# Turned probabilities, blocks and a layernorm dealt out differently in the last batch of a fused attention kernel

## The chip, the cores and the metric

The kernel runs on one core of one Trainium2 chip. The time is what the device needs for one launch, in microseconds; three runs of the kernel before gave 2748.12 us as their median (2746.18 to 2751.13). One launch computes four layers in a row, on eight batches of 512 rows by 512 columns, all in float32.

The engines are named as in the profile: PE is TensorE (its weight loads are shown apart as PEld), DVE is VectorE, ACT is ScalarE, POOL is GpSimd, SP is SyncE, whose queue issues most DMAs. Each engine works through its own instructions in order.

## The reference, cut to what matters

```python
x = L0(x, A_grid, B_grid, dt)        # derivatives of x * A, x * B on a 512 x 512 grid; relu
x = L1(x, mask, timestep, bias, Wq, Wk, Wv, Wo, W1, W2, ...)   # 16 heads of 32
    x = ln(x) * (1 + scale) + shift
    q, k, v = x @ Wq + bq, x @ Wk + bk, x @ Wv + bv
    probs = softmax(where(mask, -inf, q @ k.T / sqrt(32) + bias))
    x = x + (probs @ v) @ Wo + bo
    x = x + gelu2((ln(x) * g2 + beta2) @ W1 + b1) @ W2 + b2
x = L2(x, ...)                       # per batch one of 8 experts: Wi, gelu, Wo, layernorm
x = L3(x, ...)                       # a low-rank response, added with a gate
```

The change touches L0 (its end, and the layernorm that opens L1), the attention of L1, and the layernorm ahead of W1 for batch 0.

## The kernel before, in words

The kernel has three stages. `grid_stage` computes L0 of batch 0. `attention_stage` computes the attention of L1 for all batches, and beside it L0 of batches 1 to 7. `mlp_stage` computes the rest, first the 8 feed-forward parts of L1, then the 8 of L2 with L3 behind each. Between the last two stages the batches lie in DRAM, in `x1d[0]` to `x1d[7]`.

**Units and steps.** Attention is cut into 128 units (b, c, r): batch b, four heads (c = 0 to 3), a quarter of the rows (r = 0 to 3). The loop at L1102 makes one step for each unit, and two more at the end. t = 4c + r is the place of a unit in its batch. In the step of unit `now`, TensorE multiplies the older units' probabilities into the context (`values`, "ctx" in the profile, in every second step, for two quarters at once), then turns (transposes) the probabilities of the unit before, `old`, head by head (`turned`, "tr"), and at the end of the step computes the scores of the next unit (`scores`, "s", one PSUM bank for each of the four heads).

The step has two slots, u = 0 and 1, of two heads each. In each slot come: the turns of `old` and their copies from PSUM to SBUF ("pt"), the softmax of `now` (on VectorE one instruction, which adds scores and bias and takes the minimum, `bt, mn <- s, bt` at L1005; on ScalarE the exponential with its sum, L1010), and then one job of `fill`. The PSUM tiles of the turns have two buffers, so turns 2 and 3 wait for copies 0 and 1. In the last steps of a head group `divide` turns the inverse sums (`rb`, in the same two buffers), ScalarE copies them (`rbs`) and VectorE makes the context `ct`. GpSimd adds the mask to the bias of the next unit (L982).

Instructions wrapped in `pin` keep the order in which the program writes them on their engine. Which engine copies a turn is settled in `turned`: head 0 of a slot goes to VectorE, except in slot 0 at t in (1, 3, 4, 5, 7, 9, 15) (and in the first half of batch 0); all else goes to ScalarE.

**The jobs of `fill`.** For batches before the last they are the q and k blocks of this batch's next head groups, the v, q and k blocks of the next batch, and the output blocks (`o_block`) of the batch before; each block is four matmuls of 128x512 in two halves, one for each slot. The last batch has no next batch: it has q blocks at t = 0, 4, 9, k blocks at 1, 6, 10 and the output blocks of batch 6 at 2, 3, 7, 8, so no block at t = 5 and from 11 on. It prepares the feed-forward of batch 0 instead: statistics at t = 8, `head_norm` (ScalarE) at 10 and 11, and one `head_turn` (a turn on TensorE, an instruction on VectorE) at each of 12 to 15.

**The grid.** L0 of batch n runs beside the attention of the batches before it. It is written as the table `GRID` (L828): row j is done in the step whose index is 16(n-1) - 8 + j, at its end, mostly on VectorE. "s0" and "s1" are the statistics of the two halves of the rows, `grid_pow` makes their inverse root on GpSimd, "n0" and "n1" are the layernorm itself: a small VectorE instruction `gsh` (L817) and two ScalarE activations of 128x512 (L821). n0 stands in row 13, which is t = 5; row 15 is t = 7. `grid_gate` lets GpSimd start its mask adds only behind the last VectorE instruction of the grid in the step before; the table's "n" and "s" entries do not set that gate.

**Loads and stores.** SP's queue carries the bias (three steps ahead), the grid's coefficients, the store of a batch's result to `x1d` (at t = 9 of the batch after) and, in the last batch, `head_load`: batch 0's result at t = 1 and the four quarters of W1 at 3, 5, 11 and behind the last step. The quarters take the homes of batches 4 to 7 in SBUF, so each waits for the store of its batch. The tiles `ct` have five buffers, the grid's coefficient tiles "gq" two and "gc" three.

Of the kernel before, what the change touches and what calls it, by code (L numbers as in the profile page):

```python
# [11 lines left out]
F32 = mybir.dt.float32  # L12
# [8 lines left out]
NB = 8  # L21
S = 512
D = 512
P = 128
# [520 lines left out]
def attention_stage(  # L545
# [12 lines left out]
    nc = tc.nc  # L558
    with ExitStack() as ctx:
        wp = ctx.enter_context(tc.tile_pool(name="aw", bufs=1, reuse_waits="tile"))  # L560
        pp = ctx.enter_context(tc.tile_pool(name="ap", bufs=2, reuse_waits="tile"))
# [63 lines left out]
        def block(out, lhsT, rhs):  # L625

            def half(h):
                for k in (2 * h, 2 * h + 1):
                    mm(out, lhsT(k), rhs(k), k == 0, k == KC - 1)
            return half  # L630
# [49 lines left out]
        def o_block(b, r, tag="m"):  # L680
            o = ps.tile([P, D], F32, name=f"o_{b}_{r}", tag=tag)
            half = block(
                o, lambda k: cts[b, k][:, r * P : (r + 1) * P], lambda k: w["Wo"][:, k, :]
            )
            yield half(0)
            yield half(1)
            pin(nc.vector.tensor_tensor(xt[b][:, r, :], o, xt[b][:, r, :], ALU.add))
# [79 lines left out]
        def grid_op(n, op):  # L767
# [60 lines left out]
        GRID = {  # L828
            0: "q0 q1", 1: "e0 | w0", 2: "c0 hh C0", 3: "+0", 4: "-0 g0", 5: "G0 |", 6: "a0 A0",
            7: "b0 B0", 8: "x0 q2", 9: "e1 | w1 c1", 10: "C1 +1", 11: "-1 g1", 12: "G1 s0",  # L830
            13: "a1 | n0 A1 b1", 14: "B1 x1", 15: "s1", 16: "n1",
        }

        def grid_sums(n, j, late=True, early=True):
# [24 lines left out]
        head, h0, hT0, wi0 = {}, {}, {}, {}  # L859

        def head_load(t):

            if t == 1:
                head["x"] = w8(wo8, "x_0")
                nc.sync.dma_start(head["x"], x1d[0])
            if t in (3, 5, 11, 16):
                g = (3, 5, 11, 16).index(t)
                wi0[g] = xp.tile([P, KC, D], F32, name=f"w1_{g}", tag=f"x{g}", bufs=1)
                load_w1(nc, wi0[g], a, g)

# [24 lines left out]
        def head_turn(c):  # L895
            hT0[c] = io.tile([P, S], F32, name=f"hT0_{c}", tag="x1", bufs=4)
            tr = ps.tile([P, R, P], F32, name=f"h0tr_{c}", tag="m")
            for r in range(R):
                tp(tr[:, r, :], h0[r][:, c * P : (c + 1) * P])
            pin(  # L900
                nc.vector.tensor_scalar(
                    hT0[c], tr.rearrange("f r p -> f (r p)"), g2[:, 0, c : c + 1],
                    g2[:, 1, c : c + 1], ALU.mult, ALU.add,
                )
            )

        def grid_early(j):
            grid_sums(1, j)
            grid_loads(1, j)

        def fill(b, t):

            n = b + 1
            jobs = []
            if b == 0:
                if t == 0:
                    homes = (("m", 1), ("tr", 2), ("tr", 2), ("ctx", 1))
                    for m in range(4):
                        jobs.append(v_block(0, m, *homes[m]))
                        jobs.append(grid_early(j) for j in (m + 3,))  # L920
                    jobs.append(grid_early(7) for _ in range(1))
                    jobs.append(mask_out(0, r) for r in (2, 3))
                elif t == 2:
                    jobs.append(add_bv() for _ in range(1))
                elif t in (3, 4, 6, 7):
                    jobs.append(x1_back(0, (3, 4, 6, 7).index(t)) for _ in range(1))
            if n == NB:
                at = dict(q=(0, 4, 9), k=(1, 6, 10), o=(2, 3, 7, 8))
                for key, f in (("q", q_block), ("k", k_block)):
                    if t in at[key]:  # L930
                        jobs.append(f(b, at[key].index(t) + 1))
                if t in at["o"]:
                    jobs.append(o_block(b - 1, at["o"].index(t)))
            elif t in (0, 4, 8):
                jobs.append(q_block(b, t // 4 + 1))
            elif t in (1, 5, 9):
                turn = (lambda c: x1_in(n, c)) if t == 9 else None
                jobs.append(k_block(b, t // 4 + 1, turn=turn))
            elif t in (2, 3, 6, 7):
                if b:  # L940
                    jobs.append(o_block(b - 1, (2, 3, 6, 7).index(t)))
            elif t == 11:
                jobs.append(q_block(n, 0))
            elif t == 13:
                jobs.append(k_block(n, 0))
            else:
                jobs.append(v_block(n, (10, 12, 14, 15).index(t)))
            if n < NB:
                if t in (11, 12, 13, 14):
                    jobs.append(x1_back(n, t - 11) for _ in range(1))  # L950
                if t >= 12:
                    jobs.append(load_mask(n, t - 12) for _ in range(1))
            elif t == 8:
                jobs.append(head_stats() for _ in range(1))
            elif t in (10, 11):
                jobs.append(head_norm(r) for r in (2 * t - 20, 2 * t - 19))
            elif t >= 12:
                jobs.append(head_turn(t - 12) for _ in range(1))
            for j in jobs:
                yield from j  # L960

# [54 lines left out]
        def turned(b, c, r, u):  # L1016

            bt = bias.pop((b, c, r, u))
            for i in range(2):
                h = 2 * u + i  # L1020
                if r % 2 == 0:
                    pts[b, c, r // 2, h] = pp.tile(
                        [P, KC, 2, P], F32, name=f"pt_{b}_{c}_{r}_{h}", tag=f"pt{h}", bufs=1
                    )
                pt = pts[b, c, r // 2, h]
                tr = ps.tile([P, KC, P], F32, name=f"tr_{b}_{c}_{r}_{h}", tag="tr", bufs=2)
                for k in range(KC):
                    tp(tr[:, k, :], bt[:, i, k * P : (k + 1) * P])
                t = 4 * c + r
                if i == 0 and not (u == 0 and (t in (1, 3, 4, 5, 7, 9, 15) or (b == 0 and t < 8))):  # L1030
                    pin(nc.vector.tensor_copy(pt[:, :, r % 2, :], tr))  # L1031
                else:
                    pin(nc.scalar.copy(pt[:, :, r % 2, :], tr))  # L1033
# [23 lines left out]
        def divide(b, c):  # L1057
            rb = ps.tile([P, R, P], F32, name=f"rb_{b}_{c}", tag="tr", bufs=2)
            for r in range(R):
                tp(rb[:, r, :], sums.pop(("w", b, c, r)).rearrange("p h d -> p (h d)"))  # L1060
            rbs = pp.tile([P, S], F32, name=f"rbs_{b}_{c}", tag="rbs", bufs=1)
            pin(nc.scalar.copy(rbs, rb.rearrange("f r p -> f (r p)")))
            ct = pp.tile([P, S], F32, name=f"ct_{b}_{c}", tag="ct", bufs=5)
            pin(
                nc.vector.tensor_tensor(
                    ct, ctxs.pop((b, c)).rearrange("f r p -> f (r p)"), rbs, ALU.mult
                )
            )
            cts[b, c] = ct
# [32 lines left out]
        for i in range(n + 2):  # L1102
            now = units[i] if i < n else None
            old = units[i - 1] if 1 <= i <= n else None
            two = units[i - 2] if i >= 2 else None
            jobs = fill(now[0], 4 * now[1] + now[2]) if now else iter(())
            grid_gate(i)
            if i + 1 < n:
                add_mask(*units[i + 1])
            grid_step(i - 1, grid_pow)  # L1110
            pair = two and two[2] % 2 == 1
            if pair:
                values(two[0], two[1], two[2] // 2)
            for u in range(2):
                if old:
                    turned(*old, u)
                if now:
                    softmax(*now, u)
                next(jobs, None)
            drain(jobs)  # L1120
            split = pair and two[2] == R - 1
            if split:
                grid_step(i, lambda n, j: grid_sums(n, j, late=False))
                divide(two[0], two[1])
            if old:
                inverse(*old)
            if i + 3 < n:
                load_bias(*units[i + 3])
            if now and now[0] == NB - 1:
                head_load(4 * now[1] + now[2])  # L1130
            if now and now[0] and now[1:] == (2, 1):
                nc.sync.dma_start(x1d[now[0] - 1], xt[now[0] - 1])
            grid_step(i, lambda n, j: grid_sums(n, j, early=not split))
            grid_step(i, grid_loads)
            if i + 1 < n:
                scores(*units[i + 1])
# [753 lines left out]
```

## Time and profile before

The profiled execution took 2746.39 us, its span, from the first to the last instruction, 2744.6 us.

| stretch (us from the start) | length | PE busy | DVE busy | ACT busy | POOL busy | granted PE clock |
|---|---|---|---|---|---|---|
| grid of batch 0, first weights: 0 to 71.2 | 71.2 | 52.8 | 52.7 | 16.2 | 26.0 | 0.93 |
| attention of batches 0 to 6: 71.2 to 968.6 | 897.4 | 884.1 | 764.8 | 616.3 | 506.8 | 1.00 |
| attention of batch 7 and its end: 968.6 to 1105.5 | 136.9 | 129.0 | 74.5 | 81.9 | 60.1 | 0.98 |
| feed-forward parts: 1105.5 to 2744.6 | 1639.1 | 1627.8 | 1007.6 | 319.7 | 912.3 | 1.00 |

A row says for how many us of the stretch each engine had an instruction running. Matmuls are pipelined, so a busy TensorE is not one at its peak. The granted clock is a share of full speed.

The steps of batch 7 begin, by their first TensorE instruction, at 968.58 (t = 0), 974.98, 983.69, 990.09, 998.36, 1004.77, 1011.79, 1018.25, 1026.52, 1032.92, 1041.63, 1048.04, 1055.49, 1061.73, 1069.85 and 1076.40 (t = 15). The two closing steps follow, the first of the last output blocks' matmuls starts at 1091.74 and the first matmul of the feed-forward at 1105.47.

### The profile page before, as it was taken

To read this page: it belongs to the slowest core of one execution; us is meant where nothing else is said; L and a number is where in the kernel's file an instruction comes from. 1 tells how busy PE (TensorE), PEld (TensorE's weight loads), DVE (VectorE), ACT (ScalarE), POOL (GpSimd) and SP (SyncE) were. 2 spreads that over 40 slices of the span, in tenths; PEclk is the share of its full clock that TensorE was granted. 3 is DMA by queue.
4 is the path that set the end of the run, shared out by engine and by line. 5 is a ranking of instruction groups with operands and counts; after the bars stand their busy time and mean duration, and the time that the engine had idled before them with its cause. 6 is when DMAs were issued, how large, how long until landed. Compare 5 with 4: busy or idle time off the path is not lost.

```text
span 2744.6 us, 39872 instructions
## 1 busy us (share of the span) xinstructions
PE 2693.7 (98%) x14662; PEld 2007.0 (73%) x14662; DVE 1899.7 (69%) x3506; ACT 1034.0 (38%) x2196; POOL 1505.3 (55%) x1091
## 2 busy tenths in 40 slices
PE   7999999999999998999999999999999999999998
PEld 4455555555555555888888888888888888888886
DVE  7888888888888655677656756665456566566564
ACT  2576767667667765211211211211121221221221
POOL 3455555555555653565555656646546636636633
PEclk9999999999999999999999999999999999999998
DMA  8765767666675544642543344253133143143120
GB/s 318 238 222 178 246 190 232 220 194 227 195 242 180 170 155 142 192 129 54 143 143 84 96 145 124 55 173 123 44 127 131 51 150 128 53 150 103 63 70 31
DMA packets 190208, 405.27 MB, mean 148 GB/s; under 512 B 24024, under 2 KB 28704, under 8 KB 183742
## 3 DMA queue, kind: packets, MB, share of 16 engines
q1 hardware_dynamic: 186202, 391.97, 42.7%
q0 software_dynamic: 3360, 10.68, 3.2%
q8 instruction: 117, 1.92, 0.3%
q14 instruction: 77, 0.63, 0.1%
q10 hardware_dynamic: 452, 0.07, 0.0%
HBM read 366.97 MB, written 31.50 MB: 145 GB/s over the span
## 4 chain that ended last, share of the span: by engine, by line
PE 92%; DVE 4%; ACT 2%; DMA 1%; issue 1%; SPq 0%; ACTq 0%; POOL 0%; DVEq 0%
PE u L1173 28%; PE y L1173 28%; PE tr L570 8%; PE s L567 5%; PE ctx L567 4%; PE pq L567 4%; PE pv L567 4%; PE o L567 4%; PE pk L567 3%; PE btr L1176 1%; DVE bt L1005 1%; PE xb L570 1%; DVE x L695 1%; PE ytr L1176 1%; ACT bt L1010 1%
## 5 line engine op out<-in xcount | busy, mean ns | idle before, releaser
L982 POOL TENSOR_TENSOR bt<-bt,mk 128x1024 f32<-128x1024 f32 x256 | 542.6, 2141 | 56.8 <-DMA bt<-in_bias 38.2
L1173 PE MATMUL y<-wo,act 128*128 128x256 f32 x2560 | 573.3, 380 | 0.0
L1173 PEld LDWEIGHTS y<-wo,act 128*128 128x128 f32 x2560 | 481.3, 190 | 70.0 <-issue 6.9
L1010 ACT ACTIVATE bt<-bt,mn 128x512 f32<-128x512 f32 x512 | 365.7, 716 | 78.6 <-DVE mn L1005 78.0
L570 PEld LDWEIGHTS tr<-ident,bt 128*128 128x128 f32 x2048 | 229.1, 141 | 153.0 <-issue 124.7
L1005 DVE CUSTOM_DVE_ANT_0 bt<-s,bt 128x512 f32<-128x512 f32 x512 | 330.8, 684 | 2.4 <-PE s L567 2.4
L1173 PE MATMUL u<-bt,wi 128*128 128x256 f32 x1440 | 330.5, 379 | 0.0
L1179 DVE TENSOR_TENSOR act<-u,u 128x512 f32<-128x512 f32 x256 | 173.3, 686 | 210.0 <-PE u L1173 132.6
L1173 PEld LDWEIGHTS u<-bt,wi 128*128 128x128 f32 x1440 | 273.5, 190 | 37.2
L570 PE MATMUL tr<-ident,bt 128*128 128x128 f32 x2048 | 276.2, 278 | 11.5 <-ACT pt L1033 9.4
L1173 PE MATMUL u<-tb,ws 128*128 128x256 f32 x1024 | 242.2, 379 | 0.0
L1033 ACT COPY pt<-tr 128x512 f32<-128x512 f32 x315 | 177.1, 581 | 159.6 <-PE tr L570 155.7
L1173 PE MATMUL y<-t,s 128*128 128x256 f32 x1024 | 234.2, 380 | 0.0
L1182 POOL TENSOR_TENSOR t<-wo,t 128x512 f32<-128x512 f32 x64 | 106.6, 1681 | 200.6 <-PE y L1173 200.5
L1173 PEld LDWEIGHTS u<-tb,ws 128*128 128x128 f32 x1024 | 194.3, 190 | 26.6 <-DVE tb L1179 0.2
L1031 DVE COPY pt<-tr 128x512 f32<-128x512 f32 x197 | 135.7, 689 | 112.7 <-PE tr L570 98.0
L1173 PEld LDWEIGHTS y<-t,s 128*128 128x128 f32 x1024 | 191.1, 190 | 24.1
L1493 ACT ACTIVATE act<-act,b 128x512 f32<-128x512 f32 x128 | 82.9, 712 | 292.9 <-DVE act L1179 292.9
L1493 ACT ACTIVATE act<-act,bi 128x512 f32<-128x512 f32 x128 | 83.8, 712 | 282.6 <-DVE act L1179 282.6
L1179 DVE TENSOR_TENSOR x<-y,x 128x512 f32<-128x512 f32 x96 | 64.5, 685 | 159.1 <-PE y L1173 105.2
L1179 DVE TENSOR_TENSOR u<-u,u 128x512 f32<-128x512 f32 x192 | 131.3, 684 | 58.2 <-PE u L1173 58.1
L567 PE MATMUL s<-kt,qt 32*128 32x512 f32 x1024 | 166.4, 640 | 2.5 <-DVE mn L1005 1.6
(316 smaller groups left out, 4250.1 us busy)
## 6 DMA issues: line engine op xcount, KB each, us to landing
bt<-in_bias SPq DMA_DIRECT2D x256, 512.0 KB
wo<-in_W SPq DMA_DIRECT2D x32, 1024.0 KB
wi<-in_Wi SPq DMA_DIRECT2D x32, 1024.0 KB
wo<-in_Wo_e SPq DMA_DIRECT2D x32, 1024.0 KB
wi<-in_W SPq DMA_DIRECT2D x28, 1024.0 KB
gq<-coef_q SPq DMA_DIRECT2D x21, 512.0 KB
x1d<-x SPq DMA_DIRECT2D x8, 1024.0 KB
x<-x1d SPq DMA_DIRECT2D x8, 1024.0 KB
```

What stands on the lines that cost most here:

```text
L567: pin(nc.tensor.matmul(out, lhsT=lhsT, rhs=rhs, start=start, stop=stop))
L570: pin(nc.tensor.transpose(out, src, ident))
L982: nc.gpsimd.tensor_tensor(bt, bt, mask[b, r][:, None, :].to_broadcast([P, 2, S]), ALU.add)
L1005: nc.vector.tensor_tensor_reduce(bt[:, i, :], ss[h], bt[:, i, :], -1.0, 3.0e38, ALU.add, ALU.min, mn)
L1010: nc.scalar.activation(bt[:, i, :], bt[:, i, :], AF.Exp, bias=mn, scale=-1.0, accum_out=sums[b, c, r][:, h : h + 1],)
L1031: pin(nc.vector.tensor_copy(pt[:, :, r % 2, :], tr))
L1033: pin(nc.scalar.copy(pt[:, :, r % 2, :], tr))
L1173: pin(nc.tensor.matmul(out, lhsT=lhsT, rhs=rhs, start=start, stop=stop))
L1176: pin(nc.tensor.transpose(out, src, idn))
L1179: pin(nc.vector.tensor_tensor(out, x, y, op))
L1182: pin(nc.gpsimd.tensor_tensor(out, x, y, op))
L1493: nc.scalar.activation(acts[g][:, k, :], acts[g][:, k, :], func, bias=bi[:, j : j + 1])
```

## The change

Four things are rearranged; no computation is added or left out.

1. n0 moves from row 13 of `GRID` to row 15, ahead of s1.
2. In the last batch a turn is copied by ScalarE only if it is head 1 of slot 0; the other three go to VectorE. The rule for the other batches is the old one.
3. The last batch's ten q, k and o blocks come out of one generator, `halves`, in the order q1, k1, q2, k2, o0, q3, k3, o1, o2, o3, one half at a time: two halves at t = 0, 7, 8, 11, 12 and 14, none at 13 and 15, one elsewhere. The turns of h come in pairs at t = 13 and 15.
4. As batch 6's output blocks end later, its store to `x1d` goes from t = 9 to t = 15, and the load of the third quarter of W1 behind it; and the last batch's `ct` tiles take the buffers "gq" and "gc", which the grid no longer uses.

```diff
-            13: "a1 | n0 A1 b1", 14: "B1 x1", 15: "s1", 16: "n1",
+            13: "a1 | A1 b1", 14: "B1 x1", 15: "n0 s1", 16: "n1",
...
-            if t in (3, 5, 11, 16):
-                g = (3, 5, 11, 16).index(t)
+            if t in (3, 5, 15, 16):
+                g = (3, 5, 15, 16).index(t)
...
+        def halves(b):
+
+            for g in (
+                q_block(b, 1), k_block(b, 1), q_block(b, 2), k_block(b, 2), o_block(b - 1, 0),
+                q_block(b, 3), k_block(b, 3), *(o_block(b - 1, r) for r in (1, 2, 3)),
+            ):
+                next(g)
+                yield
+                for _ in g:
+                    pass
+                yield
...
             if n == NB:
-                at = dict(q=(0, 4, 9), k=(1, 6, 10), o=(2, 3, 7, 8))
-                for key, f in (("q", q_block), ("k", k_block)):
-                    if t in at[key]:
-                        jobs.append(f(b, at[key].index(t) + 1))
-                if t in at["o"]:
-                    jobs.append(o_block(b - 1, at["o"].index(t)))
+                if t == 0:
+                    head["fill"] = halves(b)
+                jobs.append(
+                    next(head["fill"], None)
+                    for _ in range({0: 2, 7: 2, 8: 2, 11: 2, 12: 2, 13: 0, 14: 2, 15: 0}.get(t, 1))
+                )
...
-            elif t >= 12:
-                jobs.append(head_turn(t - 12) for _ in range(1))
+            elif t in (13, 15):
+                jobs.append(head_turn(c) for c in (t - 13, t - 12))
...
-                if i == 0 and not (u == 0 and (t in (1, 3, 4, 5, 7, 9, 15) or (b == 0 and t < 8))):
+                scalar = i == 1 or (
+                    u == 0 and (t in (1, 3, 4, 5, 7, 9, 15) or (b == 0 and t < 8))
+                )
+                if b == NB - 1:
+                    scalar = i == 1 and u == 0
+                if not scalar:
                     pin(nc.vector.tensor_copy(pt[:, :, r % 2, :], tr))
                 else:
                     pin(nc.scalar.copy(pt[:, :, r % 2, :], tr))
...
-            ct = pp.tile([P, S], F32, name=f"ct_{b}_{c}", tag="ct", bufs=5)
+
+            tag, bufs = (("gq", 2), ("gc", 3))[c // 2] if b == NB - 1 else ("ct", 5)
+            ct = pp.tile([P, S], F32, name=f"ct_{b}_{c}", tag=tag, bufs=bufs)
...
+            if now and now[0] and now[1:] == ((2, 1) if now[0] < NB - 1 else (3, 3)):
+                nc.sync.dma_start(x1d[now[0] - 1], xt[now[0] - 1])
             if now and now[0] == NB - 1:
                 head_load(4 * now[1] + now[2])
-            if now and now[0] and now[1:] == (2, 1):
-                nc.sync.dma_start(x1d[now[0] - 1], xt[now[0] - 1])
```

## The prediction

> **What bounds the kernel now.** The page comes first. Its first part shows a kernel bound by TensorE; its groups give the price of the three operations that the change trades.
>
> ```profile
> PE 2693.7 (98%) x14662; PEld 2007.0 (73%) x14662; DVE 1899.7 (69%) x3506; ACT 1034.0 (38%) x2196; POOL 1505.3 (55%) x1091
> ...
> L1005 DVE CUSTOM_DVE_ANT_0 bt<-s,bt 128x512 f32<-128x512 f32 x512 | 330.8, 684 | 2.4 <-PE s L567 2.4
> ...
> L1033 ACT COPY pt<-tr 128x512 f32<-128x512 f32 x315 | 177.1, 581 | 159.6 <-PE tr L570 155.7
> ...
> L1031 DVE COPY pt<-tr 128x512 f32<-128x512 f32 x197 | 135.7, 689 | 112.7 <-PE tr L570 98.0
> ```
>
> The softmax minimum takes 684 ns on VectorE, a copy of turned probabilities 689 ns there and 581 ns on ScalarE. The shares are means over stages, so the second view is a table of stretches, one for each step of the last batch; I number its steps t=0 to 15. A step starts with its first TensorE instruction: "ctx" in odd steps, "tr" in even ones.
>
> ```profile
> core 0: us, PE busy (x) PEld busy (x) DVE busy (x) ACT busy (x) POOL busy (x), PEclk, DMA share, GB/s
> ...
> 1018.25:1026.52 8.27, 8.27 (x69) 4.35 (x65) 4.59 (x12) 4.86 (x13) 3.31 (x2) 1.00 0.43 126
> 1026.52:1032.92 6.40, 6.40 (x36) 3.40 (x32) 4.18 (x11) 4.73 (x12) 0.00 (x0) 1.00 0.55 161
> ...
> 1048.04:1055.49 7.45, 6.87 (x61) 3.66 (x57) 3.82 (x11) 5.99 (x14) 6.66 (x4) 1.00 0.92 338
> 1055.49:1061.73 6.24, 5.43 (x29) 3.06 (x28) 4.54 (x12) 5.65 (x15) 5.16 (x3) 1.00 0.74 224
> ...
> 1082.42:1087.03 4.61, 2.94 (x17) 2.40 (x17) 1.82 (x7) 2.67 (x7) 0.00 (x0) 0.70 0.02 5
> 1087.03:1091.25 4.22, 4.22 (x34) 2.07 (x33) 0.03 (x1) 0.78 (x2) 0.00 (x0) 0.52 0.00 0
> ```
>
> A step with a whole q, k or o block (t=7, 8) keeps TensorE full and takes 8.27 (odd) or 6.40 us (even). Steps t=11, 12 have no block, so some 3.4 us less of matmuls, and still take 7.45 and 6.24. So something else bounds a step at about the same length. The third view, VectorE's instructions in order of time in t=8, shows what:
>
> ```profile
> 1026.71 0.69 DVE L1005 CUSTOM_DVE_ANT_0 bt<-s,bt 128x512 f32<-128x512 f32 x1 [0.39 <-PE s L567]
> ...
> 1027.33 0.69 DVE L1005 CUSTOM_DVE_ANT_0 bt<-s,bt 128x512 f32<-128x512 f32 x1
> ...
> 1029.81 0.69 DVE L1031 COPY pt<-tr 128x512 f32<-128x512 f32 x1 [1.78 <-PE tr L570]
> 1030.41 0.68 DVE L1005 CUSTOM_DVE_ANT_0 bt<-s,bt 128x512 f32<-128x512 f32 x1
> ...
> 1031.02 0.69 DVE L1005 CUSTOM_DVE_ANT_0 bt<-s,bt 128x512 f32<-128x512 f32 x1
> ```
>
> **The loop of a step.** Back to back, VectorE starts one of these each 0.60 to 0.62 us. The third turn starts 2.65 us into the step (two turns 0.93, a half block 1.72), its copy 0.64 later, then two minima; the last ends 5.19 in. Score matmul 3 of the next unit needs that minimum (its bank). In t=14 the minimum ends at 1075.29, that matmul is issued at 1075.34 and the next step starts at 1076.40: 0.05 and 1.06. In t=8 TensorE itself reaches the scores at 5.33, so VectorE is 0.1 us early: the cover is that thin.
>
> **Part 1, turned probabilities of the last batch.** The order of instructions shows 23 copies leave ScalarE for VectorE (25 become 48); each step copies turns 0, 2 and 3 on VectorE, in the order copy 0, min 0, min 1, copy 2, copy 3, min 2, min 3. Copies 2 and 3 both stand ahead of minima 2 and 3. So with a half block in the first slot the last minimum ends at 5.19 + 0.60 = 5.79, and an even step lasts 5.79 + 0.05 + 1.06 = **6.90**; an odd one has 1.87 us of ctx ahead, **8.77**. The freed 0.58 us of ScalarE buys nothing: exponentials wait for minima. Copy 0 (ready 0.69 in, then min 0, 1 until 2.6) hides under the 2.65 until turn 2; if it did not, up to 0.7 more a step.
>
> A rule speaks against this move: the Trainium skill, "Advanced Engine Details and Errata", section "The Read-Write Bubble", says that ScalarE is nearer to PSUM and VectorE nearer to SBUF. The rows agree, 581 against 689 ns. Priced by the rule alone, the swap costs 23 x 0.11 = 2.5 us of engine time, maybe none on the path. Priced by its place, 14 steps carry a third copy at 0.60 = 8.4 us, less the thin cover. I take the place.
>
> **Part 2, blocks by halves.** It adds no matmul. Halves: two in t=0, 7, 8, 11, 12, 14, none in 13, 15, else one, always in the first slot, ahead of turns 2 and 3. Thus even a one-half step has turn 2 at 2.65, and 6.90 / 8.77 holds for it although its matmuls would need only 4.69 / 6.55; for two halves TensorE needs 6.40 / 8.27, also less than the loop. Extra: in t=4 q2's eviction falls between min 1 and copy 2 (half ends 2.81, eviction starts 2.85, next op 3.52 instead of 3.29): +0.23, 7.13. In t=13 a turn of h (0.60 us) replaces the half, but its eviction (0.72 from start to start in t=14) holds copy 2 to 3.24: end 5.69, 8.70 with ctx. The statistics in t=8 (3.2 us), `ct` and late evictions run after the last minimum and delay only copy 0, under its cover.
>
> Sum t=1 to 14: 6 x 8.77 + 8.70 + 6 x 6.90 + 7.13 = 109.85. Before: 1076.40 - 974.98 = 101.42. **+8.4 us.** t=0 turns the batch before by the old rule: 0.
>
> **Part 3, the tail.** From t=15 to the first o matmul took 15.34 us. Redone with the new order: copy 2 of unit 15 done at 5.8, so the last unit's turns start 5.85 in (6.02 before); min 3, h's eviction and `rs` to 8.4, copy 0 to 9.1, turn 2 at 9.13 (8.75 before); copies 2 and 3 now both on VectorE end at 11.1 (11.31 before, on ScalarE). About -0.2. The last two rows above show the granted clock at 0.70 and 0.52. The Trainium skill, "TensorE: Matmul & The Clock Gate", Part 1, puts the half clock behind an idle window of about 3.4 us; here the longest idle piece was 1.67 us and the clock fell all the same, so the page's condition is too narrow. By the page the new tail (idle pieces up to 2.2) would run at full clock, 1.7 us shorter; by the row it falls again, and if later, up to 1.7 us of the o matmuls are hit. I take the row: 0, both ends kept.
>
> **Part 4, n0 two steps later.** In batches 1 to 6 step t=6 loses TensorE time to it:
>
> ```profile
> 892.13 0.68 DVE L1005 CUSTOM_DVE_ANT_0 bt<-s,bt 128x512 f32<-128x512 f32 x1
> 892.26 1.07 PE L570 MATMUL tr<-ident,bt 128*128 128x128 f32 x8 [0.70 <-ACT pt L1033]
> ```
>
> ScalarE's two activations (1.52) stood ahead of both first copies; t=6 took 7.61 instead of 6.40. But VectorE in that step is back to back from 889.12 (`ct`, rs, gsh, grid ops 1.13 each, then minima) until 895.25, and the scores end 1.11 later at 896.36. When the 0.70 goes, that wait stands in its place: the gain is gsh's 0.05. Batch 0 gives 0.2 (an idle 0.16 of VectorE). At its new place, end of t=7, gsh meets GpSimd's four mask adds (8.43 us from 900.59). It took 0.13 us 13 times of 14, but 1.24 when an add was running, ending with that add. Here it would wait 0.4 (904.41 to the add's end at 904.81); VectorE has 0.64 idle in t=8: hidden. The activations end about 906.5, copies 907.05 and 907.6, just ahead of turns at 907.33 and 907.8. **-0.5**, ends -6.0 (7 x 0.86, if the gap were the whole loss) and +11 (gsh misses one add).
>
> **Part 5, DMA.** x1d[6] is stored at the end of t=15, after o3, and w1_2 waits for it on SP. Queued behind are only the b2 row, x1d[7], the Gram-Schmidt inputs and w1_3: no bias load. x1d[7]'s store to w1_3's issue took 4.34 us before, so w1_2 is issued some 4 us into t=15; GpSimd first reads it 11.6 us into the MLP (1117.10 - 1105.47), over 20 us later. `ct` in the grid's idle buffers: no wait. h turned in pairs: counted. Cost 0; without cover, a few us.
>
> **Sum.** +8.4 - 0.5 - 0.1 = +7.8 us on the profiled 2746.39 (span 2744.6 and 1.79 around it) = 2754.2. The median shown is 1.73 higher; on it, 2755.9.
>
> **Rivals.**
> - The copy hides and TensorE's work decides: then one-half steps fall to 4.69 / 6.55 (0.53 more with rb), t=1 to 14 to 88.9: -12.5, 2735. It decides if the last minimum ends before TensorE reaches the scores, 3.6 us into an even one-half step; seven VectorE ops at 0.61 need 4.3 alone. For it: the empty steps' idle is real. 0.06.
> - n0's gap is the whole loss (-6): 2750, no change. Against it: the back-to-back row. 0.12.
> - gsh loses the race with an add in each batch: 2.1 later, less 0.8 cover, 1.3 to 1.7 each: 2766. Against it: the one case seen was granted at the add's end. 0.07.
> - The change doesn't do what it says: excluded by the order (VectorE +23 rows, ScalarE -23).
>
> **The numbers.** Forecast 0.75, own range 2752 to 2759 (tail clock 1.7 each way, copies 0.52 to 0.69). 0.2%, what a measurement can tell, is 5.5 us. Forecast lies above it but for 0.05. So faster 0.06, same 0.17, slower 0.77. Range 2748.5 to 2761 leaves out the first and third rival and some edges.
>
> **What would show it.** Right: steps of about 6.9 and 8.8 us from t=1 to 14, scores waiting for DVE mn in each; t=6 of batches 1 to 6 still near 7.5 with the wait moved from ACT pt to DVE mn. Wrong: one-half steps near 4.7 / 6.6, t=6 at 6.4, or mask adds and gsh of over 1 us at t=7.

## The result and the profile after

| | before | after |
|---|---|---|
| median of 5 runs | 2748.12 us (2746.18 to 2751.13) | 2760.66 us (2756.26 to 2760.98) |
| profiled execution | 2746.39, span 2744.6 | 2756.26, span 2754.5 |
| mean granted clock | 0.994 | 0.993 |

The ratio is 1.0036, 95% interval 1.0025 to 1.0047: slower by 0.36%, or 9.9 us from profile to profile and 12.5 between the medians. The forecast was 2756.0, in a range of 2748.5 to 2761.0.

First the page of after: busy time of the engines, and the groups that answer to those shown of before.

```profile
PE 2708.8 (98%) x14662; PEld 2012.7 (73%) x14662; DVE 1919.5 (70%) x3529; ACT 1022.2 (37%) x2173; POOL 1505.6 (55%) x1091
...
L1017 DVE CUSTOM_DVE_ANT_0 bt<-s,bt 128x512 f32<-128x512 f32 x512 | 330.8, 683 | 1.3 <-PE s L567 1.3
...
L1048 DVE COPY pt<-tr 128x512 f32<-128x512 f32 x220 | 149.9, 688 | 109.8 <-PE tr L570 101.5
L1050 ACT COPY pt<-tr 128x512 f32<-128x512 f32 x292 | 164.7, 582 | 156.3 <-PE tr L570 153.2
```

The 23 copies have moved (197 to 220, 315 to 292) at unchanged durations. TensorE has the same 14662 instructions and is busy 15.1 us longer. A busy engine that does the same work in more time is either waiting inside a group of matmuls or clocked lower. The table of stretches, one row a step of the last batch, tells the two apart.

```profile
core 0: us, PE busy (x) PEld busy (x) DVE busy (x) ACT busy (x) POOL busy (x), PEclk, DMA share, GB/s
...
998.91:1007.72 8.81, 8.10 (x29) 4.09 (x28) 5.16 (x13) 3.81 (x11) 4.74 (x3) 0.81 0.43 122
...
1016.49:1023.38 6.89, 6.40 (x29) 3.32 (x28) 5.17 (x14) 4.86 (x13) 4.33 (x3) 1.00 0.51 154
1023.38:1033.82 10.44, 10.44 (x66) 5.17 (x65) 5.10 (x13) 3.82 (x11) 2.53 (x2) 0.84 0.34 100
1033.82:1040.71 6.89, 6.89 (x33) 3.69 (x32) 5.52 (x13) 3.65 (x10) 0.00 (x0) 1.00 0.50 153
...
1092.00:1095.40 3.40, 1.99 (x13) 1.26 (x12) 3.40 (x10) 1.79 (x7) 0.00 (x0) 1.00 0.93 307
1095.40:1098.80 3.40, 2.02 (x16) 1.15 (x17) 2.59 (x6) 1.48 (x5) 0.00 (x0) 1.00 0.22 84
```

These are t=4, 6, 7 and 8 and two pieces of the tail. Even steps take 6.89 whether they hold one half block (t=6) or two (t=8): what bounds them isn't TensorE's work. Steps t=4 and t=7 are longer than their like by 1.9 and 1.7 us, and there the clock is 0.81 and 0.84. In the tail, where it had been 0.70 and 0.52, it is 1.00. (A granted clock between 0.5 and 1 in a row is a mean: in these traces it is always either full or half.) VectorE's instructions in order of time, in t=10, show the bound:

```profile
1052.76 1.29 DVE L1048 COPY pt<-tr 128x512 f32<-128x512 f32 x2 [0.38 <-PE tr L570]
1053.97 0.68 DVE L1017 CUSTOM_DVE_ANT_0 bt<-s,bt 128x512 f32<-128x512 f32 x1
...
1054.57 0.69 DVE L1017 CUSTOM_DVE_ANT_0 bt<-s,bt 128x512 f32<-128x512 f32 x1
```

The step started at 1049.48. Copies 2 and 3 run one after the other from 3.28 on, and only then come minima 2 and 3; the last ends 5.78 into the step (5.19 before). TensorE's timeline shows the wait for it, and what follows such a wait:

```profile
997.25 1.73 PE L567 MATMUL s<-kt,qt 32*128 32x512 f32 x4 [0.49 <-DVE mn L1017]
998.91 1.37 PE L570 MATMUL tr<-ident,bt 128*128 128x128 f32 x8
1000.08 3.34 PE L567 MATMUL pq<-x,Wq 128*128 128x512 f32 x4
...
1023.38 3.60 PE L567 MATMUL ctx<-pt,v 128*32 128x256 f32 x32
```

Four score matmuls are spread over 1.73 us; then the four matmuls of pq take 3.34 instead of 1.88, and in t=7 ctx takes 3.60 instead of 1.93: the granted clock is at half for one stretch of 3.41 us each, called half clock below.

Where the 9.9 us between the profiles are: t=1 to 14 took 113.15 us (before 101.42), of which 3.35 are the excess of the two low-clock steps (1.68 of t=4 over its forecast 7.13, 1.67 of t=7 over 8.77), so **+8.4 for the loop and +3.4 for the clock**; the tail from t=15 to the first o matmul is 13.48 (15.34), **-1.9**; the last batch begins **0.5** earlier; from the MLP's first matmul to the end it is **0.5** longer. 8.4 + 3.35 - 1.9 - 0.5 + 0.5 = 9.9.

### The profile page after: what moved, and what is told of

The parts are those of the page before. It is cut to its first block, busy times and chain, and to the rows that moved or that the text cites. A ratio compares the mean times of both kernels' runs of the same rounds, so it can differ in the third digit from the quotient of the medians.

```text
span 2754.5 us, 39872 instructions
## 1 busy us (share of the span) xinstructions
PE 2708.8 (98%) x14662; PEld 2012.7 (73%) x14662; DVE 1919.5 (70%) x3529; ACT 1022.2 (37%) x2173; POOL 1505.6 (55%) x1091
## 4 chain that ended last, share of the span: by engine, by line
PE 95%; DVE 3%; DMA 1%; issue 0%; ACT 0%; SPq 0%; ACTq 0%; POOL 0%; DVEq 0%
PE u L1192 28%; PE y L1192 28%; PE tr L570 8%; PE s L567 6%; PE ctx L567 4%; PE o L567 4%; PE pq L567 4%; PE pk L567 4%; PE pv L567 3%; PE btr L1195 1%; PE l L251 1%; PE rb L570 1%; PE ytr L1195 1%; PE xb L570 1%; DVE bt L1017 0%; DMA a<-in_A 0%
## 5 line engine op out<-in xcount | busy, mean ns | idle before, releaser
L1048 DVE COPY pt<-tr 128x512 f32<-128x512 f32 x220 | 149.9, 688 | 109.8 <-PE tr L570 101.5
L1050 ACT COPY pt<-tr 128x512 f32<-128x512 f32 x292 | 164.7, 582 | 156.3 <-PE tr L570 153.2
L567 PE MATMUL s<-kt,qt 32*128 32x512 f32 x1024 | 181.3, 643 | 3.5 <-DVE mn L1017 2.7
```

What stands on the lines that cost most here:

```text
L567: pin(nc.tensor.matmul(out, lhsT=lhsT, rhs=rhs, start=start, stop=stop))
```

## The experiments

Each ratio below is to runs of the kernel before on the same chip (2749.6 to 2749.9 us), with its 95% interval.

**Parts alone.** Three kernels take one part of the change each. The copies on the kernel before:

```diff
-                if i == 0 and not (u == 0 and (t in (1, 3, 4, 5, 7, 9, 15) or (b == 0 and t < 8))):
+                scalar = i == 1 or (
+                    u == 0 and (t in (1, 3, 4, 5, 7, 9, 15) or (b == 0 and t < 8))
+                )
+                if b == NB - 1:
+                    scalar = i == 1 and u == 0
+                if not scalar:
```

> The kernel before with part 1 alone: in the last batch the copies of turns 0, 2 and 3 go to VectorE and that of turn 1 to ScalarE; whole blocks, n0, the order of turned h as before. Loop theory (copy 3 stands ahead of the last two minima): about +6.5 us over the kernel before, from steps with a block at 6.9 (even) and 8.8 us (odd) instead of 6.4 and 8.3, and from the steps without a block (t=5, 11 to 14), where VectorE is the bound already, each about 0.6 longer; up to 5 more or less if the clock's half windows fall elsewhere. Rival (dealing the blocks by halves is what costs): no difference, within 1 us of the kernel before.

Measured: 2755.57 us, 1.0022 (1.0013 to 1.0031), +5.7. Its t=1 to 14 took 110.54 us: 8.77 and 6.90 in most steps with a block, 7.99 in t=5 (7.02 before). Half clock left the tail and fell in t=11 to 14 (three stretches). The copies cost without any halves.

The halves, on the changed kernel (copies and n0 undone):

```diff
-            13: "a1 | A1 b1", 14: "B1 x1", 15: "n0 s1", 16: "n1",
+            13: "a1 | n0 A1 b1", 14: "B1 x1", 15: "s1", 16: "n1",
...
-                scalar = i == 1 or (
-                    u == 0 and (t in (1, 3, 4, 5, 7, 9, 15) or (b == 0 and t < 8))
-                )
-                if b == NB - 1:
-                    scalar = i == 1 and u == 0
-                if not scalar:
+                if i == 0 and not (u == 0 and (t in (1, 3, 4, 5, 7, 9, 15) or (b == 0 and t < 8))):
```

> The changed kernel with the copies of the last batch by the old rule and n0 back at its old step, so the blocks by halves (with h turned in pairs, ct in the grid's buffers and the later store of x1d) alone. Loop theory: steps of about 6.3 and 8.2 us with one half, 6.4 and 8.3 with two, so about +0.5 us over t=1 to 14 and over the kernel before; the evenly filled steps may keep the clock up in the tail, up to 1.9 us less. Rival (halves are the cost): +8 us.

Measured: 2746.32 us, 0.9987 (0.9979 to 0.9996), a gain of 3.6. Steps of 6.30 and 8.17 with one half (6.52 in t=4), 6.40 and 8.27 with two; t=1 to 14 took 101.95 us, 0.53 over before as expected. No half clock fell in the last batch, and the runs spread over 2.4 us instead of 6.7. At the same mean clock, 0.994, the runs of the kernel before took 2746.7 us on average and those of this kernel 2746.3; but only 7 of 47 runs of the kernel before had a clock of 0.994 or more, and 9 of these 13. So dealing the blocks evenly pays through the clock, by more than was allowed for, and the price lies elsewhere.

n0 alone, on the kernel before:

```diff
-            13: "a1 | n0 A1 b1", 14: "B1 x1", 15: "s1", 16: "n1",
+            13: "a1 | A1 b1", 14: "B1 x1", 15: "n0 s1", 16: "n1",
```

> The kernel before with part 4 alone, n0 two steps later. Theory: -0.5 us, because the wait of 0.70 for the two first copies is replaced by one for VectorE's minima; step t=6 of batches 1 to 6 stays near 7.5 us. Rival (the gap was the whole loss): -6 us, t=6 at 6.4 to 6.8.

Measured: 2748.25 us, 0.9995 (0.9987 to 1.0004): no difference that can be told, and -6 (0.9978) lies outside. Step t=6 took 7.54 us (7.61 before). In the changed kernel the same step of batch 6 shows where the wait went:

```profile
891.00 1.04 PE L570 MATMUL tr<-ident,bt 128*128 128x128 f32 x8
...
893.68 2.28 PE L567 MATMUL s<-kt,qt 32*128 32x512 f32 x8
...
893.49 0.68 DVE L1017 CUSTOM_DVE_ANT_0 bt<-s,bt 128x512 f32<-128x512 f32 x1
...
894.09 0.69 DVE L1017 CUSTOM_DVE_ANT_0 bt<-s,bt 128x512 f32<-128x512 f32 x1
```

The turns no longer wait for ScalarE's copies (0.70 before). The scores, which take 1.14 us where nothing holds them up, are drawn out to 2.28, while VectorE is still at minima 2 and 3; they end 1.18 us after the last minimum.

The parts don't add up: +5.7, -3.6 and -1.6 make +0.5, while the whole change comes to +9.9 by its ratio (1.0036, from another set of runs). The steps show how they work against each other. Halves win nothing where the loop of VectorE is the bound: they put a half block ahead of turn 2 in the formerly empty steps too (t=5 8.77 instead of 7.99), and with the same work spread thin over longer steps the half clock appears in t=4 and t=7.

**Place or amount.** Copy 3 back on ScalarE, copy 0 stays moved:

```diff
                 if b == NB - 1:
-                    scalar = i == 1 and u == 0
+                    scalar = i == 1
```

> The changed kernel with the copy of turn 3 of the last batch back on ScalarE: 16 of the 23 moved copies go back, the other 7 (turn 0) stay on VectorE. Place theory (only what stands ahead of the last two minima costs): steps of 6.3 and 8.2, the whole 8 us go, within 1.5 us of the kernel before. Amount theory (VectorE's load costs wherever it stands): 7 of 23 of the loss stay, +3 to +4 us.

Measured: 2745.77 us, 0.9987 (0.9981 to 0.9994). The loop takes as long as with the halves alone, to 0.01 us (101.95), so the seven copies of turn 0 cost nothing, and the sixteen of turn 3 cost it all. The time is 4.1 below the kernel before, more than the 1.5 expected, because no half clock fell in the last batch here either. VectorE's timeline of t=10, which starts at 1042.66 here:

```profile
1045.94 0.69 DVE L1048 COPY pt<-tr 128x512 f32<-128x512 f32 x1 [0.38 <-PE tr L570]
1046.55 0.68 DVE L1017 CUSTOM_DVE_ANT_0 bt<-s,bt 128x512 f32<-128x512 f32 x1
...
1047.16 0.69 DVE L1017 CUSTOM_DVE_ANT_0 bt<-s,bt 128x512 f32<-128x512 f32 x1
```

Copy 2 starts 3.28 into the step as in the changed kernel, but the first late minimum at 3.89 instead of 4.49: one copy less ahead of it, 0.60.

The other way round, all copies stay on VectorE and only their order changes:

```diff
-                    pin(nc.vector.tensor_copy(pt[:, :, r % 2, :], tr))
+                    copy = lambda pt=pt, tr=tr: pin(nc.vector.tensor_copy(pt[:, :, r % 2, :], tr))
...
+                if u == 1 and not scalar and b == NB - 1:
+                    late.append(copy)
+                else:
+                    copy()
...
                 if now:
                     softmax(*now, u)
+                for copy in late:
+                    copy()
```

> The changed kernel with one order turned round: in the last batch VectorE takes the minima of heads 2 and 3 ahead of the copies of turns 2 and 3, with the same copies on the same engines. Loop theory: the scores no longer wait for copies, a one-half step falls toward TensorE's own 4.7 (even) and 6.6 us (odd), t=1 to 14 to some 92 us instead of 113, no half clock there: about -10 us against the kernel before (2738 to 2742). Rival (VectorE's amount of work, 48 copies, is the cost): no gain over the changed kernel, +8 to +11 us against the kernel before.

Measured: 2742.21 us, 0.9976 (0.9967 to 0.9985), 7.4 below the kernel before with the very copies that had cost 8: it is their place, not VectorE's load. The size was too hopeful: t=1 to 14 took 98.6 us, not 92. Even one-half steps came to 4.93 (t=4 to 5.93), odd ones stayed at 6.9 to 8.4, and half clock fell in t=13 and 14 and again in the tail.

The same order in all batches (the condition without `b == NB - 1`):

> As the run before, with the minima of heads 2 and 3 ahead of the copy of turn 2 in all eight batches. Where TensorE is full nothing changes; in step t=6, which waits for VectorE's minima since n0 was moved, the wait gets 0.6 shorter in seven batches: 0 to -4 us against the run with the last batch alone. Rival: the later copies hold up ctx in the odd steps, up to +0.6 in each of some 50 steps, so slower by several us.

Measured: 2733.11 us, 0.9942 (0.9928 to 0.9955). That is 9 us less than with the last batch alone, where at most 4 were expected: a batch of 1 to 6 takes 124.51 us instead of 125.78, because t=2 falls from 7.54 to 6.54 as well as t=6 to 6.59; t=7 gives 0.6 back. In t=2 the scores had waited for the same minima, behind two of the grid's operations on VectorE; the expectation had reckoned with t=6 only. What still holds odd steps up is seen in TensorE's timeline of t=1:

```profile
972.60 1.04 PE L570 MATMUL tr<-ident,bt 128*128 128x128 f32 x8
974.49 0.66 PE L570 MATMUL rb<-ident,rw 128*128 128x128 f32 x4 [0.85 <-DVE pt L1048]
975.07 1.14 PE L567 MATMUL s<-kt,qt 32*128 32x512 f32 x8
```

and in VectorE's:

```profile
973.13 0.69 DVE L1017 CUSTOM_DVE_ANT_0 bt<-s,bt 128x512 f32<-128x512 f32 x1
...
973.75 1.28 DVE L1048 COPY pt<-tr 128x512 f32<-128x512 f32 x2
```

The scores follow without a wait now, but rb needs a bank of the turns, and those are freed by the two copies that were put last. That asks for one late copy instead of two.

**The best version.** Order first in all batches, and copy 3 of the last batch on ScalarE (both edits above):

> Minima of heads 2 and 3 first in all batches, and the copy of turn 3 of the last batch back on ScalarE. In the run with the order alone, the turn of the row sums (rb) waited 0.8 us in odd steps for the last of two late copies on VectorE, and ctx is next in line. Theory: with one late copy instead of two these waits shrink by up to 0.6 in the odd steps, -1 to -4 us against that run, 2729 to 2732. Rival: copy 3 now stands ahead of the exponentials of heads 2 and 3 on ScalarE, and what is won is lost to late turns: no difference, or +1 to +2.

Measured: 2729.42 us, 0.9932 (0.9919 to 0.9946): 20 us below the kernel before and 3.7 below the last run (on another chip; the intervals overlap, and so, barely, do the single runs, 2728.62 to 2731.17 against 2730.86 to 2734.24). Its rb of t=1 still waits:

```profile
972.15 0.66 PE L570 MATMUL rb<-ident,rw 128*128 128x128 f32 x4 [0.73 <-ACT pt L1050]
```

now for ScalarE, and t=1 is only 0.12 shorter, while t=2 grew by 0.17. Between the two profiles, 4.9 us apart, t=1 to 14 gave 1.7, mostly in t=9 (8.38 to 7.97) and t=13 (8.72 to 7.59), and the tail 1.6, where the half clock is gone. Another 2.2 lie ahead of the last batch, where the two kernels are alike and half clock lasted 3.4 us instead of 6.8 in batch 0: that part is luck. The MLP took back 0.6. So the time lies within what was expected, but the waits that the expectation named gave little of it.

**What the halves are worth then.** The order alone on the kernel before, in the last batch and in all:

> The kernel before with the minima of heads 2 and 3 of the last batch ahead of the copy of turn 2, nothing else. It tells what the blocks by halves are good for. Loop theory: only the steps without a block (t=5, 11 to 14) can get shorter, until ScalarE (5.7 to 6 us of work in t=11 and 12) bounds them: -3 to -5 us; but TensorE has little work in these steps, and half windows of the clock will fall there and give back 1.7 us each. Rival (halves don't matter): as far below the kernel before as the changed kernel with this order, -10 us.

> The kernel before with one change, the minima of heads 2 and 3 ahead of VectorE's copy of turn 2 in all batches: whole blocks, old copies, old n0. With the run of the same order on the changed kernel with copy 3 on ScalarE it tells what the blocks by halves are worth once the order is right. Theory: batches 1 to 6 as there, 1.2 us less each and about 8 in sum, the last batch as in the run with that order in the last batch alone (-6): -14 us against the kernel before, so 6 us are left to the halves, mostly because steps without a block are bounded by ScalarE's work. Rival (the order alone is all): -20 us.

Measured: 2743.74 us, 0.9981 (0.9975 to 0.9988) and 2734.70, 0.9944 (0.9930 to 0.9957): -5.9 (a little more than the 3 to 5 expected) and -15.0. The empty steps got shorter by 0.6 each (t=11 6.85, t=12 5.65, t=13 7.59, t=14 5.88), and one stretch of half clock fell in the tail of each. The step after the empty t=5 grew by the 0.6 that t=5 had lost (t=6 7.07). So the order is worth 15 us, and the halves with copies that don't stand in the way some 3 to 5 more (0.9932 against 0.9944, 2729.42 against 2734.70; these intervals overlap too, but the single runs do not: 2728.62 to 2731.17 against 2733.15 to 2735.55).

**n0 once more.** Its gap, so the argument went, was hidden under the late minima. With the order first in all batches, n0 went back to its old step:

> Minima of heads 2 and 3 first in all batches, with n0 at its old step. Theory: moving n0 won little because VectorE's minima were as late as ScalarE's copies; with the minima no longer late, the old place costs its gap again in t=6, 0.7 to 1.0 us in each of seven batches: +5 to +7 us against the run with n0 moved. Rival (n0's place never matters): within 1 us of it.

Measured: 2734.09 us, 0.9947 (0.9934 to 0.9961), against 0.9942 with n0 moved: the rival was right. The wait for ScalarE's first copies is back in t=6 of batch 6, but it is 0.35 long, and a batch takes 124.58 us (124.51). The first line below is from t=6 with n0 in its old place, the second from t=7 with it moved:

```profile
883.47 1.06 PE L570 MATMUL tr<-ident,bt 128*128 128x128 f32 x8 [0.35 <-ACT pt L1050]
...
894.32 0.66 PE L570 MATMUL tr<-ident,bt 128*128 128x128 f32 x4 [0.43 <-ACT pt L1050]
```

Step t=6 takes 6.94 and t=7 8.63 with n0 in its old place, 6.59 and 8.92 with it moved. The move shifts a third of a microsecond from one step to the next.

**The clock.** Is the 3.4 us of t=4 and t=7 a matter of the clock, and can work in the waits prevent it? Twelve transposes of the identity (1.4 us) were added to the steps with at most one half, into banks that the scores overwrite. At first they stood between the score matmuls:

```diff
+                if b == NB - 1 and i < 3 and 4 * c + r in (2, 3, 4, 5, 6, 7, 10, 11, 14):
+                    for k in range(KC):
+                        tp(s[:, k * P : (k + 1) * P], ident)
                 mm(
                     s, qs[b, c][o : o + HD, r * P : (r + 1) * P], ks[b, c][o : o + HD, :],
...
```

> The changed kernel with 12 more transposes of the identity (1.4 us) ahead of the first three score matmuls of each step with at most one half block in t=1 to 13, written to banks that the scores then overwrite. They stand where TensorE would wait for VectorE. Theory (the second part of the loss is the clock, halved after a stretch with little work in the array): the steps stay at 6.9 and 8.8, no half windows in t=4 and t=7, so -2 to -4 us against the changed kernel, some 2754.5 at a small spread. Rival (more work on the busiest engine costs its time): 9 x 1.4, +12 us; or no change, if the clock isn't set by the amount of work.

Measured: 2772.21 us, 1.0084 (1.0071 to 1.0098), about 13 us over the changed kernel by the ratios, as the rival said; but most of the nine steps had grown by 1.5 to 2.5 us, more than the 1.4 that was added, and TensorE's timeline shows why:

```profile
990.37 1.04 PE L570 MATMUL tr<-ident,bt 128*128 128x128 f32 x8
991.24 0.60 PE L570 MATMUL s<-ident 128*128 128x128 f32 x4
991.77 1.12 PE L567 MATMUL s<-kt,qt 32*128 32x512 f32 x2
992.82 0.66 PE L570 MATMUL s<-ident 128*128 128x128 f32 x4
993.41 1.12 PE L567 MATMUL s<-kt,qt 32*128 32x512 f32 x2
```

One head's score (x2) takes 1.12 us, and all four (x8) took 1.14: on 32 rows each they run beside each other, which the transposes between them forbid. The experiment measured that, not the clock. With all twelve ahead of the first score:

```diff
+            warm = b == NB - 1 and 4 * c + r in (2, 3, 4, 5, 6, 7, 10, 11, 14)
...
+            for i in range(3 * warm):
+                for k in range(KC):
+                    tp(two[i % 2][:, k * P : (k + 1) * P], ident)
             for i in range(4):
...
```

> The changed kernel with the 12 transposes of the identity again, now all ahead of the first score matmul of the step (in the banks of heads 0 and 1, which are free early), so that the four score matmuls still run beside each other. Clock theory: TensorE is through with them at about 5.0 us into an even step, before the last minimum at 5.8; the steps stay at 6.9 and 8.8, no stretch of t=1 to 13 has little work, no half windows there: -2 to -4.5 us against the changed kernel, 2756 to 2758.5. Rival: each step gets longer by the added 1.4 us, +12 us.

Measured: 2755.62 us, 1.0024 (1.0014 to 1.0034), some 3.3 below the changed kernel by the ratios, spread over 1.4 us instead of 4.7. The intervals overlap (up to 1.0034 here, from 1.0025 there), so the times alone are weak; the steps decide:

```profile
998.41 1.47 PE L570 MATMUL s<-ident 128*128 128x128 f32 x12
999.81 2.04 PE L567 MATMUL s<-kt,qt 32*128 32x512 f32 x8
1001.79 0.44 PE L570 MATMUL tr<-ident,bt 128*128 128x128 f32 x2
```

This is t=3. The added work ends before the last score's minimum and the step stays at 8.77. All of t=1 to 14 took 110.20 us, against 113.15 without it; t=4 takes 7.11 and t=7 8.77, at full clock. The two profiled executions nevertheless took the same time (2756.22 and 2756.26), because the last batch began 2.8 us later in this one, behind batches in which the two kernels are alike. So the steps show that more work on the busiest engine made the last batch shorter, by 2.9 us; that the whole kernel gains as much rests on the ratios.

## Why the prediction was right, and where its size was off

- **The loop (part 1).** Right, and to the tenth: 109.85 us were forecast for t=1 to 14. Take the clock's 3.35 off the measured 113.15 and 109.80 remain; with the clock kept up, 110.20. Even steps 6.89, odd 8.77, t=13 8.71. That place and not engine time sets the price is shown from both sides, by copy 3 alone (all the loss goes with it) and by the order (the copies stay, the loss goes). The Trainium skill's "The Read-Write Bubble" ("Advanced Engine Details and Errata") names the right direction, 582 ns on ScalarE against 688 here, but priced by it the part would have cost 2.5 us at most.
- **Halves (part 2).** "6.90 / 8.77 holds for it" was right. t=4 was forecast at 7.13 and is 7.11 where the clock stays up.
- **The tail (part 3): the step that failed is the one on the clock.** The forecast took the row of the old tail, expected the half clock there again and set 0. It left the tail, 1.9 us shorter, and went to two places in the loop, 3.35 us longer. Net +1.5 in the profile. For the tail the branch that was not taken gave the right number: by the idle window of the Trainium skill ("TensorE: Matmul & The Clock Gate", Part 1) the tail was to run at full clock, 1.7 shorter, and 0.2 came from the new order. But that condition does not give the loop, where TensorE idled for 0.49 us in each of the two stretches ahead of half clock. Why the clock stayed up in this tail is open. The row was the right witness against the condition of an idle window, but I read it as a property of the tail, not of the amount of work, and never asked it of the steps that the same sum had just stretched.
- **n0 (part 4).** The mechanism was right: t=6 takes 7.54 and waits for the minima instead of the copies, and a batch of 1 to 6 takes 125.78 us instead of 125.85, some 0.4 in all, where the forecast had 0.3 for these batches and 0.2 for batch 0. That the last batch also begins 0.49 earlier is luck: over the ten profiles with the old order in batches 0 to 6 it begins at 968.1 to 970.9, and most of that spread is in batch 0, where the half clock that falls there lasted 6.8 us in all six profiles with n0 moved and 3.4 in the four without. Whether n0's place does that isn't shown. gsh took 0.43 us at its new place in batches 1 to 6 (0.4 forecast) and 1.60 in batch 0; GpSimd's adds did not cost a step. The reason given, that only VectorE's lateness hid a larger gain, fell: with the minima early, n0's place is worth 0.07 us a batch.
- **DMA (part 5).** No wait for the later store showed. Up to 1631 us into the MLP its matmuls come 0.2 us earlier than before; the 0.5 by which the MLP is longer arise in its last 8 us, where half clock falls in both. What makes the difference there isn't shown; over all 14 profiles the MLP takes 1639.0 to 1640.0.
- **The sum.** 2754.2 for the profiled execution, measured 2756.26; 2755.9 for the median, measured 2760.66. That is 0.3 inside the upper end of the range, and outside the narrower 2752 to 2759 that went with the forecast. The first gap of 2.1 is the clock (+1.5) and the MLP (+0.5). The second is wider because the profiled run of after was the fastest of its five: the others ran at a mean clock of 0.991 or 0.992 against 0.993. A thousandth of the mean over 2750 us is 5.5 us at half clock, 2.75 us of TensorE's work, so by this estimate the step from 0.993 to 0.991 is worth up to 5.5; it was 4.4 to 4.7. I carried the 1.73 us between profile and median of before over; in after this distance was 4.4. Over the 47 later runs of before, with a median of 2749.89, it would have been 3.5: the profiled run of before was a fast one as well.
- **Rivals.** "The copy hides and TensorE's work decides" came true only once the order was changed, and "n0's gap is the whole loss" is refuted by n0 alone. The third, gsh losing its race with an add in each batch, did not come: 0.43 us in each of batches 1 to 6.

## What to carry to other kernels

Price an instruction that moves to another engine by what stands behind it there: here sixteen copies of 0.6 us cost 8 us ahead of the minima that TensorE waits for; behind them the kernel was faster than without the change. Before giving a step less work, look whether the work bounds it; where a loop through another engine does, turn the order in that loop first (15 us here, in the kernel before, for one order turned round). And when a change makes TensorE wait, expect a second price in its clock, which depends on how thinly the array is used and not only on idle time.

## What was not expected of the hardware

**The clock follows the array's work in fixed stretches.** The half clock always begins and ends on a grid of 3.413 us. I summed, for every stretch of that grid in the last batch of all 14 profiles, the columns that matmuls streamed, each weighed by the share of the 128x128 array in use (a score matmul on 32 rows counts a quarter, a transpose in full; a matmul across a border counts by its share on each side; eight full 128x512 matmuls, 4096, fill a stretch). Some of it:

```
profile                    stretch from   columns   next stretch
before                        1074.0        1648      full
before                        1080.9        1024      half
changed kernel                 996.2        1447      half
changed kernel                1020.1        1111      half
changed kernel                1013.2        1620      full
changed kernel                1095.2        1366      full (the exception)
copies alone                  1074.1        1412      half
halves alone                  1082.1        1536      full
spare work between scores     1108.8        1481      half
spare work ahead of scores    1092.1        1536      full
```

At full clock, 14 of the 15 stretches with fewer than 1500 columns were followed by half clock, and none with 1512 or more was. So in these traces the line lies near 36% of the array's full work. The same sum over the rest of the 14 executions, from 60 us on, agrees: at full clock, 39 more stretches had fewer than 1460, all of them followed by half clock, and none with 1530 or more was. Unweighted columns do not tell the two kinds apart, and neither does the sum without the transposes or the time that TensorE was busy. The order alone on the kernel before shows it best, in the stretch from 1071.3, with 1326 columns:

```profile
1072.66 1.73 PE L567 MATMUL s<-kt,qt 32*128 32x512 f32 x4 [0.21 <-DVE mn L1005]
1074.33 3.31 PE L567 MATMUL ctx<-pt,v 128*32 128x256 f32 x32
```

TensorE stood idle for 0.21 us of that stretch and ctx behind it took 3.31 us instead of 1.93, at half clock; with the spare work ahead of the scores it was idle for 1.5 us in the stretch from 1092.1, and the clock stayed full. The Trainium skill ("TensorE: Matmul & The Clock Gate", Part 1) names an idle window of about 3.4 us, which fits the length of the stretch but not the condition.

**Spare work can pay.** 1.4 us of useless transposes in each of nine waits cost at most 0.1 us a step and kept the clock up; put between the four score matmuls, the same work cost up to 2.5 us a step, since it ended their running side by side (1.14 us for four, 1.12 for one).
